# Spreading the experts' factors over the partitions: by a transfer from DRAM instead of by TensorE

## The chip, the cores and the metric

The kernel runs on one core of a Trainium2 chip. The metric is the time of one execution on the device in microseconds; the runs shown are three of the same kernel, and one further execution was profiled. A core has TensorE (PE; its loads of weights are shown apart as PEld), VectorE (DVE), ScalarE (ACT), GpSimd (POOL) and SyncE (SP, which here only issues transfers). SBUF is the memory on the core, PSUM the one that TensorE writes.

## What is computed

Four layers, each of an attention and a mixture or a gated network, each followed by a residual sum and a layer norm, for 1024 tokens of width 256. The change concerns the last mixture and the routing that prepares it:

```python
logits = jnp.dot(h, router_w.T)                      # 1024 x 64 experts
probs = jax.nn.softmax(logits, axis=-1)
top_vals, top_idx = lax.top_k(probs, 8)
top_vals = top_vals / jnp.sum(top_vals, axis=-1, keepdims=True)
comb = jnp.zeros((T, E)).at[jnp.arange(T)[:, None], top_idx].add(top_vals)
def body(acc, xs):                                   # over the 64 experts
    wgu, wd, w_e = xs                                # 64 units each
    g, u = jnp.split(jnp.dot(h, wgu.T), 2, axis=-1)
    eo = jnp.dot(jax.nn.silu(g) * u, wd.T)
    return (acc + eo * w_e[:, None], None)
shared = sigmoid(h @ shared_expert_gate_w.T) * ((silu(h @ sg.T) * (h @ su.T)) @ sd.T)
x = _layernorm(x + expert_out + shared)
```

The kernel computes all experts for all tokens, each hidden unit multiplied by the factor that its expert has for that token (zero where the expert isn't among the 8). The gate of the shared expert is a 65th factor.

## The kernel before

The tokens are eight tiles of 128; two halves of 512 columns serve as the moving operand. The hidden units lie on the partitions: a chunk is a pair of experts (2 x 64 units), the 33rd chunk is the shared expert (64 units). A unit of work, `add_up(i, half)` in `ffn`, makes gate and up of one chunk for one half (line 159, two fp32 matmuls each), calls `hidden`, and adds the product with the down weights to the accumulators (line 307, two fp32 matmuls). The profile shows each fp32 matmul as two records. `ffn` runs the first half of chunk i and then the second half of chunk i - LAG, with LAG = 3.

**Factors.** While the attention ends, `close(t)` finishes two token tiles at a time (t = 0, 2, 4, 6): norm, transposes (line 178), router matmuls (line 166), softmax, top 8, and the factors `comb`. It is a generator of 11 steps. `close_on` runs one step per unit of the attention, one closing after the other; what is left is run by `ffn` through its argument `before`, one step after each gate and each up, and all the rest when i = LAG - 1 is through (the flush). The last steps split the factors into three bfloat16 parts (`split3`, lines 363 to 365, on VectorE; two groups of 33 factors) and transpose them (`transpose_comb`, line 353) into `combT`, two tiles of 99 rows (3 parts x 33) and 1024 columns.

**Spread.** In `hidden`, a unit needs the factor of its expert on each of its 64 partitions. GpSimd copies columns of a selection matrix (line 2249), and one bfloat16 matmul with it as weights (`spread`, line 1100) adds the three parts up and puts each factor on its 64 partitions, in a bank of PSUM. ScalarE computes Silu of the gate (line 2255), VectorE multiplies by up (line 2256) and by the factors (line 2257).

**Buffers and order.** PSUM has four banks for gate, up and spread, and four for the accumulators. The weights come by transfers on SP's queue into a pool `w` of 10 tiles, of which `combT` holds two. The order of the instructions in the attention is the written one on all engines, SP too; in the last mixture a scheduler orders each engine's instructions at compile time by the program's order and by what is ready in its model. So line 307 of a unit stands behind the gate of the next one. Each engine runs its own list in order.

Of the kernel before, what the change touches and what calls it, by code (L numbers as in the profile page):

```python
# [24 lines left out]
BF16 = mybir.dt.bfloat16  # L25
# [3 lines left out]
ALU = mybir.AluOpType  # L29
AX = mybir.AxisListType  # L30

P = 128
T = 1024
# [3 lines left out]
HALF = 512  # L37
# [5 lines left out]
class Kit:  # L43
# [242 lines left out]

    LAG = 3

    def ffn(self, chunks, count, hidden, before=iter(())):

        nc = self.nc
        acc = [self.wide() for _ in range(NC)]
        held = {}

        def add_up(i, half):
            size, gate, up, down, more = held[i] if half == 0 else held.pop(i)
            g, u = self.bank()[:size], self.bank()[:size]  # L300
            self.project(g, gate, half * HALF, HALF)
            next(before, None)
            self.project(u, up, half * HALF, HALF)
            next(before, None)
            h = hidden(g, u, half, more)
            for m in range(NC):
                nc.tensor.matmul(  # L307
                    acc[m][:, half * HALF : (half + 1) * HALF],
                    lhsT=down[:, m * P : (m + 1) * P], rhs=h, start=i == 0, stop=i == count - 1,
                )  # L310

        for i in range(count + self.LAG):
            if i < count:
                held[i] = next(chunks)
                add_up(i, 0)
            if i == self.LAG - 1:
                for _ in before:
                    pass
            if i == count - 1:
                self.add_ffn(acc, 0)  # L320
            if i >= self.LAG:
                add_up(i - self.LAG, 1)
        self.add_ffn(acc, 1)

    def add_ffn(self, acc, half, scale=None):
# [19 lines left out]
                )  # L345
        self.norm_half(half)

    def transpose_comb(self, parts, combT, t):

        n = combT.shape[0]  # L350
        ps = self.bank()[:n, : 2 * P]
        for i in range(2):
            self.nc.tensor.transpose(
                ps[:, i * P : (i + 1) * P], parts[:, i].rearrange("p s e -> p (s e)"), self.ident
            )
        self.nc.vector.tensor_copy(combT[:, t * P : (t + 2) * P], ps)

    def split3(self, parts, x, shape):

        nc = self.nc  # L360
        short = self.tile("st", shape, BF16, tag="short", bufs=2)
        for i in range(2):
            nc.vector.tensor_copy(short, x)
            nc.vector.tensor_copy(parts[i], short)
            nc.vector.tensor_tensor(parts[2], x, short, ALU.subtract)
            x = parts[2]

    def selector(self, n):

        t = self.tile("st", [3 * n, n], BF16, tag=f"select{n}", bufs=1)  # L370
        for i in range(3):

            cols = self.ident[: 3 * n, i * n : (i + 1) * n]
            if i == 0:
                self.nc.gpsimd.tensor_copy(t, cols)
            else:
                self.nc.gpsimd.tensor_tensor(t, t, cols, ALU.add)
        return t

class Pair:  # L380

# [67 lines left out]
class Pipe:  # L449
# [6 lines left out]
    LAG = 5  # L456
# [436 lines left out]
def ffn0(k, a):  # L893
# [198 lines left out]
                if not late and tile_ + 2 < len(ternary_tiles):  # L1092
                    next(ternary_tiles[tile_ + 2])
    k.moe = results, slots, prob


def spread(k, select, combT, half):

    by = k.bank()[: select.shape[1]]
    k.nc.tensor.matmul(  # L1100
        by, lhsT=select, rhs=combT[:, half * HALF : (half + 1) * HALF], start=True, stop=True
    )
    return by


def attn1(k, a):
# [832 lines left out]
def attn3(k, a):  # L1939

    nc = k.nc
# [21 lines left out]
    for _ in load(0):  # L1963
# [4 lines left out]
        out=wr[:, :, :64], in_=a["L3_ffn_router_w"].rearrange("(c p) e -> p c e", p=P)  # L1968
    )
    nc.sync.dma_start(out=wr[:, :, 64], in_=a["L3_ffn_shared_expert_gate_w"])  # L1970
    k.combT = [k.tile("w", [99, T], BF16) for _ in range(2)]
    k.closing, stats = [], {}

    def close(t):
# [26 lines left out]
        for i in range(2):  # L2001
# [6 lines left out]
        nc.vector.tensor_reduce(total, probs, axis=AX.X, op=ALU.add)  # L2008
        nc.vector.reciprocal(inv, total)


        comb = k.tile("t2", [P, 2, 2, 33])
        nc.vector.tensor_tensor(
            comb[:, :, :, :32], probs.rearrange("p t (g e) -> p t g e", g=2),
            inv.unsqueeze(2).unsqueeze(3).to_broadcast([P, 2, 2, 32]), ALU.mult,
        )
        nc.gpsimd.memset(comb[:, :, 0, 32], 0.0)
        nc.vector.tensor_scalar(gate, gate, 1.0, None, ALU.add)
        nc.vector.reciprocal(comb[:, :, 1, 32], gate)
        parts = [k.tile("t2", [P, 2, 3, 33]) for _ in range(2)]  # L2020
        for group in range(2):
            yield
            k.split3(
                [parts[group][:, :, i, :] for i in range(3)], comb[:, :, group, :], [P, 2, 33]
            )
        for group in range(2):
            yield
            k.transpose_comb(parts[group], k.combT[group], t)

    def close_on():  # L2030
        if k.closing and next(k.closing[0], k) is k:
# [182 lines left out]
def ffn3(k, a):  # L2214


    nc = k.nc
    select = k.selector(33)

    def chunks():  # L2220
        gu = wd = None
        for p in range(32):
            if p % 2 == 0:
                gu = k.weights(
                    [P, NC, 512],
                    a["L3_ffn_gate_up"][:, p * 256 : (p + 2) * 256].rearrange(
                        "(c p) f -> p c f", p=P
                    ),
                )
            if p % 4 == 0:  # L2230
                wd = k.weights([P, 4, D], a["L3_ffn_down"][:, p * D : (p + 4) * D])
            at = (p % 2) * 256
            yield (
                P, lambda c, w=gu, s=slice(at, at + P): w[:, c, s],
                lambda c, w=gu, s=slice(at + P, at + 2 * P): w[:, c, s], wd[:, p % 4, :], p,
            )
        gu = k.weights([P, NC, P], a["L3_ffn_shared_gate_up"].rearrange("(c p) f -> p c f", p=P))
        wd = k.weights([64, D], a["L3_ffn_shared_down"])
        yield (64, lambda c: gu[:, c, :64], lambda c: gu[:, c, 64:], wd, 32)

    chosen = {}

    def hidden(g, u, half, p):
        n = g.shape[0]
        group, at = (1, 32) if n == 64 else (p // 16, p % 16 * 2)
        if half == 0:

            chosen[p] = k.tile("t2", [99, n], BF16, tag="t1", bufs=4)
            nc.gpsimd.tensor_copy(  # L2249
                chosen[p].rearrange("r (e u) -> r e u", u=64),  # L2250
                select[:, at : at + n // 64].unsqueeze(2).to_broadcast([99, n // 64, 64]),
            )
        by = spread(k, chosen[p], k.combT[group], half)
        s, h = (k.tile("t2", [P, HALF])[:n] for _ in range(2))
        nc.scalar.activation(s, g, AF.Silu)  # L2255
        nc.vector.tensor_tensor(h, s, u, ALU.mult)  # L2256
        nc.vector.tensor_tensor(h, by, h, ALU.mult)
        return h

    k.ffn(chunks(), 33, hidden, (step for steps in k.closing for step in steps))  # L2260


STAGES = (attn0, ffn0, attn1, ffn1, attn2, ffn2, attn3, ffn3)
# [5 lines left out]
    attn2: dict(wide=3, q=4, k=4, v=2, pt=3, ot=6, tops=2, parts=6),  # L2269
    ffn2: dict(p4=3, t2=8),  # L2270
    attn3: dict(q=12, k=4, v=8, pt=2, p4=2, turned=2, ot=3, t2=4, raw=2),
    ffn3: dict(p4=4, t2=8),
}


# [89 lines left out]
```

## Time and profile before

| | |
|---|---|
| runs shown | 2253.94, 2241.89, 2248.37 us; median 2248.37 |
| profiled execution | 2254.7 us, span of its profile 2253.0 us |
| mean granted clock of TensorE | 0.962 |
| busy over the span | PE 2060.1 us (91%), DVE 1306.5 (58%), ACT 851.0 (38%), POOL 532.1 (24%) |
| transfers | 169.57 MB, mean 75 GB/s; SP's queue 24.9% of 16 engines' span |
| last mixture | from 1868 us to the end |

The page gives the busy time of each engine, the span in 40 slices, the transfers, the chain of work that ended last, and the costliest groups of instructions by line. A row of the timeline is: start, duration, engine, line, operation, output and inputs with their shapes, count, and in brackets the idle time before it with what ended it. Matmuls are pipelined and overlap in it; the distance between starts is the time that one costs. A row of the table of windows is: the window, its length, then busy time and number of instructions of PE, PEld, DVE, ACT and POOL, the granted clock, the mean busy share of the 16 DMA engines, and GB/s. A row of the transfers is: output and input, queue, kind, count, KB of each, and the median time from issue to landing.

### The profile page before, as it was taken

How to read it: one execution, taken by the hardware profiler on the slowest of the kernel's cores; microseconds unless marked ns; L12 is line 12 of the kernel's file. 1: busy time of each engine (PE TensorE's matmuls, PEld its weight loads, DVE VectorE, ACT ScalarE, POOL GpSimd, SP SyncE). 2: the span in 40 equal slices, each digit the busy share in tenths (PEclk: the TensorE clock that was granted, in tenths of full speed). 3: DMA queues.
4: the chain of work that ended last, by engine and by line, in shares of the span. 5: the costliest groups of instructions: out<-in, count | busy, mean ns of one | idle time of the engine just before them, and what ended most of it. 6: DMA issues, size and time to landing. Idle time of an engine off the chain costs nothing.

```text
span 2253.0 us, 24727 instructions
## 1 busy us (share of the span) xinstructions
PE 2060.1 (91%) x7967; PEld 1211.3 (54%) x7967; DVE 1306.5 (58%) x2640; ACT 851.0 (38%) x2232; POOL 532.1 (24%) x811
## 2 busy tenths in 40 slices
PE   7988777899999997988988998899999988999997
PEld 4656544566666665754444443466666664444443
DVE  6898756577777664555664445277777664222223
ACT  3656424443444433444353222654444432111111
POOL 5343132233333323312110000333333320000000
PEclk9999879899999998989999999999999999999998
DMA  6322543154546543015000000044444330111100
GB/s 184 72 71 57 145 125 107 49 144 109 145 100 159 142 104 83 24 43 169 11 2 10 29 28 2 24 94 110 92 106 98 75 106 19 38 37 47 31 1 19
DMA packets 143728, 169.57 MB, mean 75 GB/s; under 512 B 31248, under 2 KB 114768, under 8 KB 143600
## 3 DMA queue, kind: packets, MB, share of 16 engines
q1 hardware_dynamic: 134016, 142.95, 24.9%
q0 software_dynamic: 9584, 25.05, 3.6%
q8 instruction: 64, 1.05, 0.2%
q14 instruction: 64, 0.52, 0.1%
HBM read 68.20 MB, written 17.17 MB: 38 GB/s over the span
## 4 chain that ended last, share of the span: by engine, by line
PE 66%; DVE 9%; ACT 3%; DMA 3%; issue 3%; POOL 2%; SPq 1%; DVEq 0%; ACTq 0%; POOLq 0%
PE bank L159 22%; PE wide L274 9%; PE bank L439 8%; PE wide L307 8%; PE bank L166 4%; DVE turned L402 2%; PE bank L1219 2%; DMA pt<-turned 2%; PE bank L887 2%; PE bank L1656 2%; PE bank L1394 1%; PE bank L1050 1%; ACT pt L1681 1%; PE wide L1669 1%; POOL p L267 1%
## 5 line engine op out<-in xcount | busy, mean ns | idle before, releaser
L159 PE MATMUL bank<-xT,w 128*128 128x512 f32 (+1 forms) x1488 | 644.9, 567 | 6.3 <-DVE xT L185 6.0
L159 PEld LDWEIGHTS bank<-xT,w 128*128 128x128 f32 x1488 | 286.5, 196 | 272.9 <-issue 248.0
L402 DVE STREAM_TRANSPOSE turned<-p 128x128 f32<-128x128 f32 (+7 forms) x232 | 283.6, 1222 | 83.3 <-DMA pt<-turned 47.5
L274 PE MATMUL wide<-k,q 128*128 128x512 f32 (+3 forms) x768 | 295.3, 494 | 18.4 <-ACT p L259 17.5
L267 POOL TENSOR_SCALAR p<-p,st 128x128 f32<-128x128 f32 (+7 forms) x256 | 190.3, 743 | 486.0 <-DVE st L266 485.4
L439 PE MATMUL bank<-pt,v 128*128 128x256 f32 x1216 | 281.5, 373 | 12.1 <-DMA pt<-turned 7.8
L439 PEld LDWEIGHTS bank<-pt,v 128*128 128x128 f32 x1216 | 227.2, 192 | 65.6 <-issue 24.2
L254 DVE TENSOR_REDUCE st<-wide 128x1 f32<-128x128 f32 (+7 forms) x256 | 193.4, 756 | 50.8 <-PE wide L279 43.8
L274 PEld LDWEIGHTS wide<-k,q 128*128 128x128 f32 x768 | 140.1, 192 | 135.8 <-issue 93.2
L307 PE MATMUL wide<-t,w 128*128 128x512 f32 x392 | 189.0, 605 | 8.0 <-DVE t L1933 4.8
L2256 DVE TENSOR_TENSOR t<-t,bank 128x512 f32<-128x512 f32 x66 | 45.3, 687 | 246.6 <-PE bank L159 246.6
L259 ACT ACTIVATE p<-wide,st,factor 128x128 f32<-128x128 f32 (+7 forms) x128 | 106.3, 830 | 214.6 <-POOL st L256 213.0
L259 ACT ACTIVATE p<-wide,st 128x128 f32<-128x128 f32 (+7 forms) x128 | 94.8, 740 | 234.9 <-DVE st L254 213.9
L2255 ACT ACTIVATE t<-bank 128x512 f32<-128x512 f32 x66 | 39.4, 597 | 292.5 <-PE bank L159 287.7
L307 PEld LDWEIGHTS wide<-t,w 128*128 128x128 f32 x392 | 68.3, 189 | 112.7 <-issue 48.3
L166 PE MATMUL bank<-w,xT 128*128 128x512 f32 (+2 forms) x288 | 118.6, 549 | 0.8 <-DVE st L266 0.8
L810 ACT ACTIVATE e<-wide,st 128x128 f32<-128x128 f32 x256 | 89.8, 376 | 75.6 <-DVE st L818 67.1
L249 DVE TENSOR_TENSOR wide<-wide,causal 128x128 f32<-128x128 f32 x192 | 55.8, 291 | 97.1 <-PE wide L274 96.0
L1681 ACT ACTIVATE pt<-wide 128x1024 f32<-128x1024 f32 (+3 forms) x96 | 75.6, 811 | 70.3 <-PE wide L1675 68.5
L2249 POOL COPY t<-select 99x128 bf16<-99x128 bf16 (+1 forms) x33 | 9.4, 291 | 318.2 <-PE bank L1100 318.2
L166 PEld LDWEIGHTS bank<-w,xT 128*128 128x128 f32 x288 | 52.6, 196 | 46.2 <-issue 40.0
L1633 DVE TENSOR_REDUCE st<-wide 128x2 f32<-128x1024 f32 x64 | 64.3, 1020 | 21.2 <-PE wide L1629 10.3
(316 smaller groups left out, 2918.1 us busy)
## 6 DMA issues: line engine op xcount, KB each, us to landing
pt<-turned SPq DMA_DIRECT2D x60, 240.0 KB, 4.8
pt<-turned SPq DMA_DIRECT2D x60, 176.0 KB, 3.5
pt<-turned SPq DMA_DIRECT2D x156, 64.0 KB, 2.1
w<-in_L_ffn_gate_up_dram SPq DMA_DIRECT2D x16, 512.0 KB, 3.7
pt<-turned SPq DMA_DIRECT2D x28, 256.0 KB, 4.8
pt<-turned SPq DMA_DIRECT2D x60, 112.0 KB, 2.9
pt<-turned SPq DMA_DIRECT2D x28, 224.0 KB, 4.2
w<-in_L_attn_Wq_dram SPq DMA_DIRECT2D x12, 512.0 KB, 3.8
```

The source lines that it names most:

```text
L159: self.nc.tensor.matmul(out, lhsT=weight(c), rhs=self.xcols(c, lo, n), start=c == 0, stop=c == NC - 1)
L166: self.nc.tensor.matmul(out, lhsT=self.xcols(c, lo, n), rhs=weight(c), start=c == 0, stop=c == NC - 1)
L254: nc.vector.tensor_reduce(top, scores[:, :n], axis=AX.X, op=ALU.max, negate=True)
L259: nc.scalar.activation(probs[:, :n], scores[:, :n], AF.Exp, bias=top, scale=1.0 if scale is None else scale, accum_out=total,)
L267: self.nc.gpsimd.tensor_scalar(probs[:, :n], probs[:, :n], total, 1.0, ALU.mult, ALU.mult)
L274: self.nc.tensor.matmul(s[:, lo : lo + m], lhsT=query, rhs=key(lo, m), start=True, stop=not masked or lo + m < n, skip_group_check=masked,)
L307: nc.tensor.matmul(acc[m][:, half * HALF : (half + 1) * HALF], lhsT=down[:, m * P : (m + 1) * P], rhs=h, start=i == 0, stop=i == count - 1,)
L402: k.nc.vector.transpose(squares.rearrange("p b (k q) -> p b k q", q=32), probs[:, :n].rearrange("p (k i b) -> p b k i", b=4, i=32),)
L439: self.k.nc.tensor.matmul(out.rearrange("p (a q) -> p a q", q=32) if first else out.rearrange("p (s a q) -> p s a q", s=2, q=32), lhsT=val ...
L810: nc.scalar.activation(e[:, r, f, b, :], sc[:, r, f, b, :], AF.Exp, bias=top[:, at : at + 1], accum_out=total[:, at : at + 1],)
L1633: nc.vector.tensor_reduce(st[:, i, :] if half else to, sc[:, :, :n], axis=AX.X, op=ALU.max, negate=True,)
L1681: nc.scalar.activation(two[:, :, lo:], sc[:, :, lo:], AF.Exp)
```

## The change

The factors stay in float32. `close` transposes them directly (65 rows: 64 experts and the shared gate) and stores them in a tensor `factors` of [65, 1024] in DRAM, by a transfer on SP's queue. The steps of splitting go; a closing has 9 steps, one of them empty. In `hidden`, a transfer on SP's queue reads the rows of the chunk's experts, repeats each over 64 partitions, and lands in a new tile `by` in SBUF, of which there are 8. `split3`, `transpose_comb`, `selector`, `spread` and `combT` go. `ffn` gets its lag as an argument, and the last mixture uses 4.

```diff
-    def ffn(self, chunks, count, hidden, before=iter(())):
+    def ffn(self, chunks, count, hidden, before=iter(()), lag=LAG):
...
-            if i == self.LAG - 1:
+            if i == lag - 1:
                 for _ in before:
                     pass
...
-            if i >= self.LAG:
-                add_up(i - self.LAG, 1)
+            if i >= lag:
+                add_up(i - lag, 1)
...
-    k.combT = [k.tile("w", [99, T], BF16) for _ in range(2)]
+    k.factors = k.tile("dram", [65, T], tag="factors")
...
-        comb = k.tile("t2", [P, 2, 2, 33])
+        comb = k.tile("t2", [P, 2, 65])
         nc.vector.tensor_tensor(
-            comb[:, :, :, :32], probs.rearrange("p t (g e) -> p t g e", g=2),
-            inv.unsqueeze(2).unsqueeze(3).to_broadcast([P, 2, 2, 32]), ALU.mult,
-        )
-        nc.gpsimd.memset(comb[:, :, 0, 32], 0.0)
+            comb[:, :, :64], probs, inv.unsqueeze(2).to_broadcast(shape), ALU.mult
+        )
         nc.vector.tensor_scalar(gate, gate, 1.0, None, ALU.add)
-        nc.vector.reciprocal(comb[:, :, 1, 32], gate)
-        parts = [k.tile("t2", [P, 2, 3, 33]) for _ in range(2)]
-        for group in range(2):
-            yield
-            k.split3(
-                [parts[group][:, :, i, :] for i in range(3)], comb[:, :, group, :], [P, 2, 33]
-            )
-        for group in range(2):
-            yield
-            k.transpose_comb(parts[group], k.combT[group], t)
+        nc.vector.reciprocal(comb[:, :, 64], gate)
+        yield
+        yield
+        ps = k.bank()[:65, : 2 * P]
+        for i in range(2):
+            nc.tensor.transpose(ps[:, i * P : (i + 1) * P], comb[:, i, :], k.ident)
+        combT = k.tile("t2", [65, 2 * P])
+        nc.vector.tensor_copy(combT, ps)
+        nc.sync.dma_start(out=k.factors[:, t * P : (t + 2) * P], in_=combT)
...
     def hidden(g, u, half, p):
         n = g.shape[0]
-        group, at = (1, 32) if n == 64 else (p // 16, p % 16 * 2)
-        if half == 0:
-            chosen[p] = k.tile("t2", [99, n], BF16, tag="t1", bufs=4)
-            nc.gpsimd.tensor_copy(
-                chosen[p].rearrange("r (e u) -> r e u", u=64),
-                select[:, at : at + n // 64].unsqueeze(2).to_broadcast([99, n // 64, 64]),
-            )
-        by = spread(k, chosen[p], k.combT[group], half)
+        by = k.tile("by", [P, HALF])[:n]
+        rows = k.factors[2 * p : 2 * p + n // 64, half * HALF : (half + 1) * HALF]
+        nc.sync.dma_start(out=by, in_=rows.unsqueeze(1).to_broadcast([n // 64, 64, HALF]))
...
-    k.ffn(chunks(), 33, hidden, (step for steps in k.closing for step in steps))
+    k.ffn(chunks(), 33, hidden, (step for steps in k.closing for step in steps), lag=4)
...
-    ffn3: dict(p4=4, t2=8),
+    ffn3: dict(p4=4, t2=8, by=8),
```

## The prediction

> **What bounds the kernel now.** I read the table of windows first, for the stage; then the timeline of one steady unit, for the wait that ends last; then the timeline of the stage's first units; then the transfers.
>
> ```profile
> 1850.00:2253.00 403.00, 382.90 (x987) 172.29 (x985) 123.40 (x275) 56.20 (x91) 11.18 (x35) 0.98 0.09 28
> ```
>
> The last mixture starts at 1868 (its first L159) and is bound by TensorE (382.9 of 403 us busy; VectorE 123, ScalarE 56, GpSimd 11, transfers 9%). So relief for GpSimd or ScalarE is worth nothing here. One unit (a pair of experts, one half of the tokens) in steady state:
>
> ```profile
> 2001.15 1.88 PE L159 MATMUL bank<-xT,w 128*128 128x512 f32 x4
> 2002.87 0.38 PE L1100 MATMUL bank<-w,t 99*128 99x512 bf16 x1
> 2003.09 1.88 PE L159 MATMUL bank<-xT,w 128*128 128x512 f32 x4
> 2003.14 0.69 DVE L2256 TENSOR_TENSOR t<-t,bank 128x512 f32<-128x512 f32 x1 [3.89 <-PE bank L159]
> 2003.93 0.69 DVE L2257 TENSOR_TENSOR t<-bank,t 128x512 f32<-128x512 f32 x1
> 2004.68 0.32 PEld L307 LDWEIGHTS wide<-t,w 128*128 128x128 f32 x2 [0.54 <-DVE t L2257]
> 2004.81 1.88 PE L307 MATMUL wide<-t,w 128*128 128x512 f32 x4
> 2006.52 1.88 PE L159 MATMUL bank<-xT,w 128*128 128x512 f32 x4
> 2008.24 0.38 PE L1100 MATMUL bank<-w,t 99*128 99x512 bf16 x1
> ```
>
> Starts count, not busy times. Four records (two fp32 matmuls) take 1.72 us from start to start; the bf16 spread (L1100) takes 0.22 (2002.87 to 2003.09), though it is shown as 0.38. A unit is 3 x 1.72 + 0.22 = 5.37 us, which is the distance between two spreads. See also how tight L307 sits: up ends at 2002.87, L2256 and L2257 follow, L307 loads its weights at 2004.68 and starts at 2004.81, at once when the next gate (started 2003.09) is through. VectorE is a second chain with almost no slack.
>
> The start of the stage holds the only long idle of TensorE:
>
> ```profile
> 1887.78 1.00 PE L166 MATMUL bank<-w,xT 128*128 128x65 f32 x8
> 1894.01 1.18 PE L353 MATMUL bank<-ident,t 128*99 128x128 f32 x4 [5.23 <-DVE t L365]
> 1894.98 6.02 PE L159 MATMUL bank<-xT,w 128*128 128x512 f32 x8
> ```
>
> The router of the last two token tiles (L166) is followed by 5.23 us in which TensorE waits for softmax, top 8 and split on VectorE, and then eight records take 6.02 us instead of 3.6.
>
> Transfers in three windows (the last two columns are the busy share of 16 DMA engines and GB/s): a plain 256 KB transfer at 448, and at 506 the two loads of scales, whose source is 8 rows, each repeated 16 times, so that its outermost dimension is 8:
>
> ```profile
> 448.00:448.50 0.50, 0.50 (x5) 0.45 (x4) 0.41 (x2) 0.00 (x0) 0.00 (x0) 1.00 0.98 377
> 506.00:506.50 0.50, 0.50 (x4) 0.45 (x3) 0.50 (x1) 0.50 (x1) 0.00 (x0) 1.00 0.50 197
> 506.50:507.00 0.50, 0.50 (x3) 0.26 (x2) 0.50 (x1) 0.50 (x3) 0.00 (x0) 1.00 0.50 132
> ```
>
> The repeated rows kept exactly half of the engines busy. A busy engine moves 377 / (0.98 x 16) = 24.0 GB/s in the plain transfer, 164.5 / 8 = 20.6 in the other.
>
> **The Trainium skill.** (1) "DMA: Bandwidth & Descriptors", section "Why a DMA increments its semaphore by 16 and not by 1": the number of engines of one DMA is the largest one up to 16 that divides the slowest dimension (other than 1) of both access patterns. The windows at 506 agree (8 of 128 partitions: 8 engines), though those were issued by GpSimd; no run yet shows a smaller one from SP. (2) "TensorE: Matmul & The Clock Gate", Part 1: after about 3.4 us idle the clock is halved until TensorE has been busy for about as long; the 6.02 us agree. (3) "VectorE: DVE Perf Modes", "Why tensor_tensor can't do 2×_2P or 4×": two fp32 tensors go at the plain rate from SBUF also. The trace agrees: 0.724 us for 128x512 with both in SBUF (L191), 0.692 for L2257 with one in PSUM.
>
> **The change, part by part.** The sum is made against the profiled execution (2254.7 us, span 2253.0), which lies 0.3% above the median 2248.37; I carry the difference over.
>
> *Spread leaves TensorE.* 66 x 0.22 = 14.2 us of issue. But L307 still waits for L2256 and L2257. From the end of up to L307's earliest start: 0.27 + 0.79 + 0.75 and about 0.12 for the weights = 1.92 us; the next gate now fills 1.72 of it. So 0.20 of the 0.22 turns into a wait for L2257, unless the scheduler puts half of the next up ahead of L307. Value: 0 to -14 us, taken -1.
>
> *GpSimd* loses 33 copies (9.4 us, hidden under 318 us of idle): nothing.
>
> *Split goes.* Per pair of tiles 12 VectorE instructions of about 0.2 us and 2 of 4 transposes go; one copy of 0.42 and one transfer of 65 KB come. Behind L166 that shortens the chain by 1.3 us (1892.7 to 1894.0). More important, a closing falls from 11 steps to 9, and lag=4 lets two more steps run before the flush. Counting steps: before, the pair t=4 enters the stage with 8 steps left and t=6 with all its router work in the flush. After, t=4 enters with 2 left, t=6 gets its router matmuls after the third unit's up, and its softmax runs beside the fourth unit's gate and up (3.4 us). The 5.23 us and the 2.4 us of half clock should mostly go: -8 us (0 to -9, since a new order may leave the wait). In the attention's tail, three split instructions (1.0 us) lie inside one wait of 2.9 us before L421: 0 to -1.
>
> *The store* sits on SP in the fixed order of the attention; it waits for the copy, and the `pt<-turned` transfers behind it wait for later work of VectorE anyway: nothing, at most 0.5 us each.
>
> *The spread by DMA.* 64 transfers of 256 KB (and two of 128 KB). Their source is [2, 64, 512]: outermost dimension 2, so by (1) **two engines of 16**, the same two each time, 128 KB each. At 24.0 GB/s that is 5.46 us, at 20.6 it is 6.36; the second rate contains a transfer's start, so I weigh 2 to 1: 5.73 us. All loads of weights pass these two engines as well:
>
> ```profile
> w<-in_L_ffn_gate_up_dram SPq DMA_DIRECT2D x12, 512.0 KB, 3.7
> w<-in_L_ffn_down_dram SPq DMA_DIRECT2D x6, 512.0 KB, 3.6
> ```
>
> 18 x 32 KB at 24.0 = 25 us. Together 64 x 5.73 + 25 = 392 us on each of the two, against 5.35 x 66 = 353 us of TensorE. Eight buffers give a lead, not a rate. The first transfer can start when the factors of tiles 0 to 3 are stored: the transposes of t=2 now lie about where its step 7 lay (1853), plus copy, store and landing: 1857; if the loads are issued only with the stage, 1868. I take 1862. Then the last pair's factors land at 1862 + 392 = 2254. After that come L2257 (0.75), two L307 (3.4) and what followed L307 before (2241.8 to 2253.0, 11.2): 15.4 us, so 2269: **+16 us**. What TensorE gained (the -1 and -8) is cover that this queue eats; it isn't added. SP issues 66 more transfers of some 0.37 us (as for gate_up), 24 us in 380; each may wait for a buffer, and weights behind it wait too, which costs no more since they share the queue.
>
> **The rivals.**
> *A, the transfer is hidden*: the framework or the queue spreads it over 16 engines (1.4 us per unit). Then TensorE's terms count: -1 - 8 - 1 = -10, to -24 where the order also removes the wait for L2257: 2224 to 2238, about 2235. For it: 9% transfer load today. Against: the half share at 506.
> *B, two engines at the plain rate from 1857*: 1857 + 64 x 5.46 + 25 = 2231, end 2247, -6: **2242, no difference**. For it: 24.0 GB/s was seen in an undisturbed transfer. The point from which the queue costs time is 5.56 us per transfer with this start (5.48 with mine).
> *C, two engines reading the same row 64 times are as slow as the loads of scales*: start 1866, 64 x 6.36 + 25 = 2298, end 2313, +60: 2309.
>
> **Numbers.** About 0.5% (11 us) is what a measurement of this kernel can tell from no change. Forecast, slower, 2264: 0.41; C 0.10; B 0.20; A 0.29. So faster 0.29, same 0.20, slower 0.51. The likeliest case alone reaches from 2255 to 2285. The range goes from 2230 (most of A) to 2300 (short of C).
>
> **What would show it.** Right: the loads of `by` take over 5 us each and keep about 2/16 = 0.13 of the engines busy through the whole stage (weights on top); L307 or L2257 waits for the transfer of `by`; the units lie 5.8 us or more apart; TensorE's idle behind L166 is gone. B: the same shares, with units near 5.5. A: landings of 2 to 4 us, units at 5.35 with L307 waiting for L2257, or at 5.15 with no wait. Wrong altogether: a tail of the attention that moved by more than 3 us, or factors that arrive late only in the first units.

## The result, and the profile after

The kernel after takes 2237.87 us (median of 20 runs) against 2248.13 us of the kernel before (20 runs): ratio 0.9952, 95% interval 0.9944 to 0.9961, so 0.5% **faster** (10.3 us by the medians, 10.8 by the ratio). The forecast was 16 us slower. The profiled execution of after took 2230.2 us (span 2228.5).

Single executions differ by more than this change: up to the last attention, TensorE's instructions are the same in both kernels, and yet the profile of after is 16.8 us ahead there (1384.4 against 1401.2). So I compare stages. From its first L159 to the end of the span, the last mixture took 384.9 us before (from 1868.13) and takes 379.8 us after (from 1848.71). The last attention takes 464.3 us against 466.9.

In the kernel after, line 2201 loads `by`, 2203 is Silu, 2204 and 2205 are the products with up and with the factors, 1981 transposes the factors; 159, 166, 178 and 307 are as before. First the window of the last mixture (columns as before: window, length, busy time of PE, PEld, DVE, ACT and POOL, clock, share of DMA engines, GB/s):

```profile
1830.00:2228.00 398.00, 375.74 (x916) 163.82 (x916) 114.82 (x223) 54.06 (x89) 2.56 (x4) 0.98 0.21 70
```

TensorE is still nearly full, and the transfers rose from 9% to 21%. The next two windows hold nothing but loads of `by`; the table of transfers counts them:

```profile
1900.00:1910.00 10.00, 10.00 (x24) 4.12 (x23) 2.76 (x4) 1.19 (x2) 0.00 (x0) 1.00 0.13 51
1950.00:1960.00 10.00, 10.00 (x24) 4.21 (x23) 2.24 (x4) 1.19 (x2) 0.00 (x0) 1.00 0.13 51
```

```profile
by<-factors SPq DMA_DIRECT2D x64, 256.0 KB
```

A share of 0.13 is 2 of 16 engines, as forecast. But these two move 51 GB/s, 25.5 each, so a transfer takes 262144 B / 51 GB/s = 5.14 us; the packet records of the trace have 5.13 us between the ends of two. I had taken 5.73.

A steady unit early in the stage (timeline, DVE, ACT and PE):

```profile
1910.04 3.60 PE L159 MATMUL bank<-xT,w 128*128 128x512 f32 x8
...
1912.02 0.69 DVE L2204 TENSOR_TENSOR t<-t,bank 128x512 f32<-128x512 f32 x1 [3.86 <-PE bank L159]
1912.74 0.69 DVE L2205 TENSOR_TENSOR t<-by,t 128x512 f32<-128x512 f32 x1
1913.49 1.98 PE L307 MATMUL wide<-t,w 128*128 128x512 f32 x4
...
1915.31 1.88 PE L159 MATMUL bank<-xT,w 128*128 128x512 f32 x4
```

Eight records are up of this unit and gate of the next. Units lie 5.27 us apart (1910.04 to 1915.31), not 5.37 and not the 5.15 of three times 1.72: L307 takes 1.82 us from start to the next start instead of 1.72, since its first load of weights stands behind the wait for L2205, which ends at 1913.43 just as the gate is through. From 1961 to 2140, while weights are loaded too, 12 of some 33 units look like this:

```profile
2006.20 0.69 DVE L2205 TENSOR_TENSOR t<-by,t 128x512 f32<-128x512 f32 x1 [1.11 <-DMA by<-factors]
2006.95 1.98 PE L307 MATMUL wide<-t,w 128*128 128x512 f32 x4 [0.94 <-DVE t L2205]
```

And the waits of the whole kernel (engine, tile, line, releaser: us in total, times, longest):

```profile
DVE t L2205 <- DMA by<-factors: 12.6, 20, 1.8
PE wide L307 <- DVE t L2205: 11.8, 14, 1.6
```

Two of the 14 waits for L2205 are no work of the queue: they are 1.56 us each, at 2184 and 2215, behind the shared expert at the end of each half, and e1 below has them too. So the queue costs TensorE 8.7 us of waits here. After 2140 there are no weights left to load, and no more of these. At the start of the stage the idle stretch is gone: the timeline has the last pair's router at 1863.42 and its transposes six microseconds later with no idle before them, at full clock:

```profile
1863.42 1.00 PE L166 MATMUL bank<-w,xT 128*128 128x65 f32 x8
1864.26 2.79 PE L159 MATMUL bank<-xT,w 128*128 128x512 f32 x6
...
1869.46 0.38 PE L1981 MATMUL bank<-ident,t 128*65 128x128 f32 x2
```

### The profile page after: what moved, and what is told of

It is laid out like the page before. It is cut to its first block, busy times and chain, and to the rows that moved or that the text cites. A ratio compares the mean times of both kernels' runs of the same rounds, so it can differ in the third digit from the quotient of the medians.

```text
span 2228.5 us, 24592 instructions
## 1 busy us (share of the span) xinstructions
PE 2037.2 (91%) x7893; PEld 1191.4 (53%) x7893; DVE 1299.4 (58%) x2588; ACT 849.6 (38%) x2230; POOL 522.3 (23%) x771
## 4 chain that ended last, share of the span: by engine, by line
PE 62%; DVE 9%; DMA 7%; ACT 3%; issue 3%; POOL 2%; SPq 1%; DVEq 0%; POOLq 0%; ACTq 0%
PE bank L159 19%; PE wide L274 9%; PE bank L408 8%; PE wide L307 6%; DMA by<-factors 5%; PE bank L166 4%; PE bank L1179 2%; DVE turned L371 2%; PE bank L1616 2%; PE bank L856 2%; PE bank L1019 1%; DMA pt<-turned 1%; PE bank L1354 1%; POOL p L267 1%; PE wide L1629 1%
## 5 line engine op out<-in xcount | busy, mean ns | idle before, releaser
L159 PE MATMUL bank<-xT,w 128*128 128x512 f32 (+2 forms) x1488 | 629.2, 563 | 4.1 <-DVE xT L185 3.0
L159 PEld LDWEIGHTS bank<-xT,w 128*128 128x128 f32 (+1 forms) x1488 | 283.1, 194 | 275.1 <-issue 254.3
L307 PE MATMUL wide<-t,w 128*128 128x512 f32 (+1 forms) x392 | 196.7, 626 | 17.0 <-DVE t L2205 11.8
L2204 DVE TENSOR_TENSOR t<-t,bank 128x512 f32<-128x512 f32 (+1 forms) x66 | 45.3, 686 | 238.8 <-PE bank L159 238.8
L2203 ACT ACTIVATE t<-bank 128x512 f32<-128x512 f32 (+1 forms) x66 | 39.4, 597 | 305.5 <-PE bank L159 279.5
L307 PEld LDWEIGHTS wide<-t,w 128*128 128x128 f32 (+1 forms) x392 | 67.8, 191 | 134.3 <-DVE t L2205 58.4
L845 PE MATMUL bank<-w,ot 128*128 128x256 f32 x256 | 67.4, 411 | 6.8 <-ACT ot L839 5.5
```

The lines of the kernel that those rows point to most:

```text
L159: self.nc.tensor.matmul(out, lhsT=weight(c), rhs=self.xcols(c, lo, n), start=c == 0, stop=c == NC - 1)
L307: nc.tensor.matmul(acc[m][:, half * HALF : (half + 1) * HALF], lhsT=down[:, m * P : (m + 1) * P], rhs=h, start=i == 0, stop=i == count - 1,)
L845: nc.tensor.matmul(y, lhsT=oT[:, i % 2 * 2 + i // 2].rearrange("p b n -> p (b n)"), rhs=wo[:, i, :], start=i == 0, stop=i == 3,)
```

## The experiments

Two figures for each kernel: the ratio to the kernel before on the same chip, and the length of the last mixture in its profile (first L159, or what stands for it, to the end of the span). "Rest" is what the time changed by outside that stage: (ratio - 1) x 2248, less the change of the stage from 384.9. Each length is that of one profiled execution; kernels that do the same in this stage agree within 1.2 us (before and e18; after and e14). The last column is where the tiles allocated in the last stages begin, in bytes past a multiple of 256 (factors / tiles of earlier stages).

| kernel | ratio, 95% | last mixture, us | rest, us | place |
|---|---|---|---|---|
| before | 1 | 384.9 | 0 | - / 160 |
| after | 0.9952 (0.9944 to 0.9961) | 379.8 | -5.7 | 0 / 0 |
| e1_sixteen | 0.9886 (0.9867 to 0.9905) | 366.1 | -6.8 | 0 / 0 |
| e2_factor_first | 0.9954 (0.9939 to 0.9970) | 378.8 | -4.2 | 0 / 0 |
| e3_both | 0.9909 (0.9890 to 0.9928) | 367.9 | -3.5 | 0 / 0 |
| e4_before_nine | 0.9984 (0.9970 to 0.9998) | 376.9 | +4.4 | - / 160 |
| e5_eleven_lag3 | 0.9977 (0.9967 to 0.9986) | 386.2 | -6.5 | 0 / 0 |
| e6_extra | 1.0122 (1.0103 to 1.0141) | 421.2 | -8.9 | 0 / 0 |
| e7_by16 | 1.0027 (1.0015 to 1.0039) | 395.5 | -4.5 | 0 / 0 |
| e8_turned | **0.9852** (0.9832 to 0.9872) | 357.6 | -6.0 | 0 / 0 |
| e9_turned_product | 0.9877 (0.9859 to 0.9896) | 366.0 | -8.8 | 0 / 0 |
| e10_turned_two | 0.9932 (0.9918 to 0.9945) | 376.4 | -6.8 | 0 / 0 |
| e12_before_lag4 | 1.0005 (0.9994 to 1.0016) | 385.7 | +0.3 | - / 160 |
| e13_two_queues | 1.0041 (1.0029 to 1.0054) | 400.8 | -6.7 | 0 / 0 |
| e14_held | 0.9956 (0.9940 to 0.9972) | 380.9 | -5.9 | 0 / 0 |
| e16_selector | 1.0016 (1.0007 to 1.0025) | 388.6 | -0.1 | 96 / 96 |
| e17_after_pad32 | 1.0041 (1.0026 to 1.0057) | 396.5 | -2.4 | 32 / 32 |
| e18_before_pad32 | 0.9996 (0.9985 to 1.0007) | 385.5 | -1.5 | - / 192 |
| e19_after_pad64 | 1.0017 (1.0008 to 1.0025) | 389.4 | -0.7 | 64 / 64 |
| e20_pad_last | 1.0023 (1.0013 to 1.0032) | 395.5 | -5.4 | 32 / 0 |

### Does the queue on two engines cost time?

**e1_sixteen**: one transfer per expert.

```diff
-        rows = k.factors[2 * p : 2 * p + n // 64, half * HALF : (half + 1) * HALF]
-        nc.sync.dma_start(out=by, in_=rows.unsqueeze(1).to_broadcast([n // 64, 64, HALF]))
+        for e in range(n // 64):
+            row = k.factors[2 * p + e : 2 * p + e + 1, half * HALF : (half + 1) * HALF]
+            nc.sync.dma_start(out=by[64 * e : 64 * e + 64], in_=row.to_broadcast([64, HALF]))
```

> The kernel after, but each expert's 64 partitions are loaded by a transfer of their own (outermost dimension 64), so that all 16 DMA engines should share it. Theory (the queue on two engines still costs time after the change): the 12.6 us in which VectorE waits for the factors vanish, units lie 5.27 us apart to the end of the stage, and the time is 9 to 12 us below the kernel after, near 2227; the share of busy engines outside the weight loads is no longer 0.13. Rival (the two-engine transfer is hidden, and its waits only stand in the place of others): within 3 us of the kernel after, near 2237.

Measured: 13.7 us less in the stage than after, and 0.9886 against 0.9952. Units lie 5.27 to 5.28 us apart to the end of the stage, VectorE never waits for `by`, and a transfer lands 2.9 us after its issue (median). The theory holds, and the effect is somewhat above the 9 to 12 us that it named. Two down matmuls one unit apart:

```profile
2001.19 1.98 PE L307 MATMUL wide<-t,w 128*128 128x512 f32 x4
2006.46 1.98 PE L307 MATMUL wide<-t,w 128*128 128x512 f32 x4
```

The view of the tile `by` has no entry under "sat idle before it":

```profile
L2202 SPq DMA_DIRECT2D by<-factors x130: 444/588/597, 1851.9 to 2170.0; - x130
L2206 DVE TENSOR_TENSOR t<-by,t x66: 678/691/693, 1867.8 to 2215.7; 128x512 f32<-128x512 f32 x64, 64x512 f32<-64x512 f32 x2
its engine sat idle before it (us, times) until:
```

**e6_extra**: the kernel after with 12% more on the same two engines.

```diff
+        more = k.tile("more", [16, HALF])[: 8 * (n // 64)]
+        nc.sync.dma_start(out=more, in_=rows.unsqueeze(1).to_broadcast([n // 64, 8, HALF]))
```

> The kernel after, with a second small transfer behind each load of the factors: the same rows onto 16 partitions of a tile that nobody reads (outermost dimension 2, 8 rows of 2 KB more on each of the same two engines), which raises the load per unit from 5.13 us to 72/64 x 5.13 = 5.77 us, about what the prediction took for it. Theory (the two engines end the stage, and the prediction failed by the size of the transfer): about 58 x 0.64 = 37 us above the kernel after less what TensorE hides, near 2268; units at 5.8 us and more. Rival (the waits for the factors have another cause, such as SP's order): less than 10 us above the kernel after.

Measured: the stage 41.4 us longer than after; the waits of VectorE for `by` go from 12.6 to 41.7 us. That is 65 us per us of transfer, about one for each of the 66 units: the queue is what ends there. With a load of 5.77 us per unit, about what I forecast for a transfer, the kernel is 27 us slower than before, more than the 16 that were forecast.

**e13_two_queues**: half of the transfers on ScalarE's queue (`(nc.sync, nc.scalar)[half].dma_start`).

> The kernel after, with the factors of the second half of the tokens loaded through ScalarE's queue and those of the first half through SP's. Open is whether a second queue's transfers of outermost dimension 2 use the same two engines. Theory 1 (the same two engines): VectorE's waits for the factors stay near 12 us or grow, since ScalarE now also waits for free buffers ahead of Silu: 0 to +8 us against the kernel after. Theory 2 (other engines, or the rate is that of the queue and not of the engines): the waits fall under 3 us, and the time is 8 to 12 us below the kernel after, near 2228.

Measured: 21 us longer than after in the stage. While transfers of both queues are under way a window still shows

```profile
1950.00:1960.00 10.00, 10.00 (x24) 4.12 (x23) 2.76 (x4) 0.60 (x1) 0.00 (x0) 1.00 0.13 51
```

that is, the same two engines. The Trainium skill, "DMA: Bandwidth & Descriptors", section "Issuing engines are not separate DMA queues", says that transfers of any issuing engine run on the same 16; this run agrees, and for a transfer of two rows it is the same 2 of the 16. The loss was larger than theory 1 allowed, since ScalarE now stands in front of Silu with a transfer that waits for a buffer (three waits of L2203 with 32.5 us in all).

**e7_by16**: `by=16` instead of `by=8`.

> The kernel after with 16 buffers for the spread factors instead of 8. Theory (rate: with the weight loads the two engines need 5.13 + 23/64 = 5.49 us a unit, against 5.27 of TensorE, and the lead is set by when the last tokens' factors are stored): no change, 0 to -3 us, waits for the factors still over 9 us. Rival (lead: the queue stood still for lack of free buffers early in the stage): the waits fall to 5 us or less, -7 us and more.

Measured: neither. The waits for `by` are gone altogether, so there was lead to be had, and the stage is 15.7 us longer. The waits list shows what came late instead:

```profile
PE bank L159 <- DMA w<-in_L_ffn_gate_up_dram: 14.0, 4, 6.2
PE wide L307 <- DMA w<-in_L_ffn_down_dram: 7.3, 1, 7.3
```

The queue gave its lead to `by`, and the weights, which stand behind in the same list, arrive late: TensorE waits 21.3 us for weights, where in after it waited 8.7 us for the factors. The rest of the 15.7 us goes with the half clock behind the longest of these waits (granted clock of the stage 0.962, against 0.980 in after). More buffers for the one load are a delay for the other where both share a bound queue.

### What did TensorE gain?

**e4_before_nine**: the kernel before, with split and spread kept, closings of 9 steps and lag=4.

```diff
+        yield
         for group in range(2):
-            yield
             k.split3(...)
+        yield
         for group in range(2):
-            yield
             k.transpose_comb(parts[group], k.combT[group], t)
...
-tag="t1", bufs=4)
+tag="t1", bufs=5)
```

> The kernel before with split and spread on TensorE, but the closings cut from 11 steps to 9 (both splits in one step, both transposes in another) and lag=4 (with five buffers for the spread 0/1 rows instead of four). Theory (the shorter closings and the later flush removed the idle stretch of TensorE at the start of the stage): the wait of 5.23 us behind the router and the half clock after it go, -8 us against the kernel before, near 2240. Rival (the idle went because the split went from VectorE): the wait stays at 3 us or more, and the time is within 3 us of the kernel before.

Measured: the stage is 8.0 us shorter, as worked out, and the wait of 5.23 us behind the router and the half clock are gone (the longest wait left at the start is 1.47 us). The whole kernel gains 3.6 us only. In its profile the attention is 7.9 us longer than before; TensorE waits there for both splits that now come in one piece, and longer for the attention's own probabilities (`p`):

```profile
1810.04 0.46 PE L353 MATMUL bank<-ident,t 128*99 128x128 f32 x2 [1.29 <-DVE t L365]
...
1854.96 1.97 PE L421 MATMUL bank<-ident,p 128*128 128x128 f32 x8 [3.42 <-POOL p L267]
```

**e12_before_lag4**: lag=4 alone.

> The kernel before with lag=4 alone (and five buffers for the spread 0/1 rows), closings of 11 steps as they were. Theory (the gain at the start of the stage needs the shorter closings, since with 11 steps the last pair's router still falls into the flush behind the fourth unit): the wait of about 5 us behind the router stays, 0 to -2 us against the kernel before. Rival (the later flush is what removes it): the wait falls below 2 us, and -6 us or more.

Measured: no gain (385.7), and the long wait is there, 6.66 us. The lag alone doesn't do it; the shorter closings are needed. Whether they would do it with lag=3 was not tried.

```profile
1892.23 1.15 PE L353 MATMUL bank<-ident,t 128*99 128x128 f32 x4 [6.66 <-DVE t L365]
```

**e5_eleven_lag3**: the kernel after with two more empty `yield` in `close` and lag=3.

> The kernel after, with two more empty steps in each closing (11 again) and lag=3 (the factors still spread by DMA). Theory (the shorter closings and the later flush are worth about 7 us at the start of the stage, whatever spreads the factors): TensorE's wait in front of the transposes of the last factors is back at 3 us or more and half clock follows; Silu of the first unit to Silu of the last takes 5 to 8 us longer than in the kernel after, or less by what the transfers then gain in lead (the waits for the factors, 12.6 us, may shrink); time 2238 to 2245. Rival (steps are worth nothing here since the queue of transfers ends the stage): within 2 us of the kernel after.

Measured: 6.4 us more in the stage, and the wait is back, though shorter than before, since no split stands in it:

```profile
1882.37 0.69 PE L1983 MATMUL bank<-ident,t 128*65 128x128 f32 x2 [3.85 <-DVE t L1972]
```

So the steps are worth 6.4 to 8.0 us on either side of the change. What else the change does to TensorE is the distance from e4 to e1: 376.9 - 366.1 = 10.8 us. Of it 66 x (5.37 - 5.275) = 6.3 us is the steady unit; the rest, 4.5 us, lies at the start of the stage, where e4 still waits for splits (1.1 us) and makes twice the transposes; how the 4.5 us divide was not measured.

### What is left in the unit: the products behind up

**e2_factor_first** multiplies Silu by the factors first and by up last (`h = by * s`, then `h * u`); **e3_both** does it on top of e1.

> The kernel after, but VectorE multiplies Silu(gate) with the factors first and with up last, so that only one VectorE instruction (0.69 us) lies between the end of up and the down matmuls. The scheduler then puts the down matmuls half a gate (0.86 us) after up, not a whole one (1.72 us). Theory (the queue on two engines binds in the later part of the stage): little, 0 to -4 us against the kernel after, with VectorE still waiting for the factors, now in the first of the two products. Rival 1 (the wait of the down matmuls for the second product is what the change is short of): units at 5.15 us and -8 us. Rival 2 (the earlier place of the down matmuls brings a new wait of about 0.2 us per unit): 0 to +6 us.

> The kernel after with both edits: one transfer per expert over 16 engines, and the factors multiplied first. Theory (queue first, the chain on VectorE second): 8 us below the variant with 16 engines alone, units at 5.15 us, near 2219. Rival (down matmuls only half a gate after up: 0.20 for up's landing + 0.69 + 0.12 for the weights against 0.86): units at 5.25 to 5.35, within 4 us of the variant with 16 engines alone, near 2227.

Measured: e2 within 0.5 us of after (0.9954 against 0.9952), e3 1.9 us longer than e1 in the stage. In both the units lie 5.34 us apart, as in e3:

```profile
2004.99 1.98 PE L307 MATMUL wide<-t,w 128*128 128x512 f32 x4
2010.33 1.98 PE L307 MATMUL wide<-t,w 128*128 128x512 f32 x4
```

The scheduler, expecting the product earlier, put L307 behind half a gate, and the new wait (5.34 - 5.15 = 0.19 us) is longer than the old one (0.13). The rival of e3 and the second of e2 were right about the units. So the order has to be held as well.

**e8_turned**: e3 with the order of the steady units written out, the down matmuls of a unit behind the whole gate of the next.

```diff
             self.project(g, gate, half * HALF, HALF)
+            while late:
+                late.pop()()          # the down matmuls of the unit before
...
+            late.append(down_matmuls)
+            if not turned[0]:
+                late.pop()()
...
+            with self.in_order():
+                turned[0] = True
+                for i in range(lag, count - 1):
+                    step(i)
```

> The variant with 16 engines, the factors multiplied before up, and the order of the steady units written out: the down matmuls of a unit stand behind the whole next gate (1.72 us after up's end). Theory (the remaining wait per unit is the chain of two VectorE products: 0.20 for up's landing + 2 x 0.75 + weights against 1.72): with one product, no wait, units at 3 x 1.715 = 5.15 us instead of 5.27, 62 x 0.13 = 8 us below the variant with 16 engines alone, near 2220. Rival (the 0.13 us is a cost of changing between matrices on TensorE that no order removes): units stay at 5.27 and the time near 2228.

Measured: units at 5.15 us, the stage 8.5 us below e1, ratio 0.9852: 33 us faster than before and 22 us faster than after, the fastest kernel of this study. The down matmuls (line 311 here) now take their 1.72 us:

```profile
2001.87 1.88 PE L311 MATMUL wide<-t,w 128*128 128x512 f32 x4
2003.58 3.60 PE L159 MATMUL bank<-xT,w 128*128 128x512 f32 x8
2007.02 1.88 PE L311 MATMUL wide<-t,w 128*128 128x512 f32 x4
```

**e9_turned_product**: the same order with up first and the factors last.

> The variant with 16 engines and the steady units' order written out as in the fastest variant so far (2215), but with VectorE's products as in the kernel after (up first, factors last, both behind up). A control for where that variant's 0.13 us a unit came from. Theory (the chain of two VectorE products behind up): units at 5.27 us as with 16 engines alone, and the time near 2228, 12 us above the fastest variant. Rival (the written order itself): units at 5.15 us, near 2216.

Measured: units at 5.27 us and a stage of 366.0 us, that of e1. So the 0.13 us is the second product behind up, and the written order by itself gives nothing.

**e10_turned_two**: e8 with the two-engine transfer of the kernel after.

> The fastest variant so far (written order, factors multiplied before up, units at 5.15 us), but with the factors loaded as in the kernel after, by one transfer on two engines. Theory (the queue of the two engines ends the stage as soon as it runs out of lead, so TensorE's gain is cover that it eats): units at 5.15 us for the first ones, then VectorE waits for the factors for 18 to 22 us in all instead of 12; the time within 4 us of the kernel after, near 2237, and 20 us above the same kernel with 16 engines. Rival (the waits depend on how units fall, not on the rate): the gain of 0.13 us a unit comes through, near 2228.

Measured: units at 5.15 us until about 1950, then about half of them come late by up to 2 us, with VectorE waiting for `by`; the stage is 376.4 us, 18.8 us above e8 and only 3.4 below after. Of the 8.5 us that the same two edits gain with 16 engines (e8 against e1), the queue eats 5.1.

### Where are the other five microseconds?

The last mixture explains -5.1 of the -10.8 us. Two things outside the last mixture differ: `combT` held two of the weight pool's ten buffers, and GpSimd built a 0/1 matrix at the start.

**e14_held**: after, with two tiles of the weight pool held to the end.

> The kernel after, with two of the weight pool's ten buffers held from the start of the last attention to the end, as the two tiles of split factors held them in the kernel before. The last mixture and the last attention account for about 7 us of the 10.7 us gained; some 4 us lie ahead of them or are spread. Theory 1 (the two freed buffers bring them): near 2242, 4 us above the kernel after. Theory 2 (they come from elsewhere): within 2 us of the kernel after, ratio to before 0.994 to 0.996.

**e16_selector**: after, with `select = k.selector(33)` kept, unread.

> The kernel after, with the 0/1 matrix of the spread still built by GpSimd (three small instructions that the scheduler puts at the start of the kernel, ahead of the masks) and read by nobody. Theory 1 (GpSimd's instructions at the start of the kernel delay the first stages): near 2242, 4 us above the kernel after. Theory 2 (they cost nothing): within 2 us of the kernel after.

Measured: the buffers are nothing (0.9956). The matrix takes all the gain away (1.0016), and not where theory 1 saw it: the last mixture is 8.8 us longer, with 19.7 us of waits for `by`, though only GpSimd's list of instructions has changed: those of TensorE, VectorE and ScalarE are the same, in the same order. What moved are the tiles. The matrix takes 96 bytes of each partition, and everything allocated later lies 96 bytes further: in the built program `by` is at 105568 instead of 105472, which is a multiple of 256 (and of 512). In the kernel before, the matrix and the small tiles of the split push the later tiles by 416 bytes, to 160 past a multiple of 256. The weights' tiles lie ahead of all these and keep their place. So the last four runs moved tiles only; the one small `memset` that comes with each costs nothing by e14, which has four of them.

```diff
+    pad = k.tile("st", [P, 8], tag="pad", bufs=1)       # e17: 32 bytes; e19: [P, 16]; e18: in the kernel before
+    nc.gpsimd.memset(pad[:, :1], 0.0)
...
-    ffn3: dict(p4=4, t2=8, by=8),
+    ffn3: dict(pad=1, p4=4, t2=8, by=8),                # e20: a pool of its own, in the last stage
```

> The kernel after, with a tile of 32 bytes per partition that nobody reads, where the 0/1 matrix of the spread lay. The instructions of every engine stay in their order (one small GpSimd memset at the start); all later tiles move by 32 bytes in SBUF, the spread factors from 105472 (a multiple of 512) to 105504 (32 over a multiple of 64), the place that they had with the 0/1 matrix kept and that the kernel before gives its tiles. Theory (placement): near 2252, as with the 0/1 matrix, ratio to before 1.000 to 1.003, with transfers of factors at 5.2 instead of 5.1 us. Rival (GpSimd's instructions, or chance): within 3 us of the kernel after, ratio 0.994 to 0.997.

> The kernel before, with an unread tile of 32 bytes per partition behind the 0/1 matrix, which moves the later tiles from 32 over a multiple of 64 to a multiple of 64 (105888 to 105920). Theory (placement costs the kernel before in its stages with many transfers into SBUF): -3 to -7 us, ratio 0.997 to 0.9985. Rival: no change, 0.999 to 1.001.

> As the kernel after with 32 bytes of padding, but 64 bytes: the later tiles stay on multiples of 64 (not of 512), and the GpSimd memset is there too. Theory (what counts is a multiple of 64): within 2 us of the kernel after, ratio 0.994 to 0.997. Rival 1 (a larger multiple counts): as with 32 bytes, 1.000 to 1.003. Rival 2 (the memset or any shift costs): likewise 1.000 and more.

> The kernel after, with the unread 32 bytes put into the pools of the last mixture only, so that the factors lie 32 bytes over a multiple of 64 and the tiles of all earlier stages lie as in the kernel after. Theory (placement acts on the queue of the factors as well as on the earlier stages): the last mixture takes 385 to 389 us as with the 0/1 matrix kept, instead of 380; 5 to 8 us above the kernel after, ratio 0.9975 to 0.999. Rival (the placement of the factors does not matter, that of earlier tiles does): within 2 us of the kernel after.

Measured: 32 bytes cost 20 us (1.0041), 64 bytes 14.6 us (1.0017). So a multiple of 64 is not enough, and e18, which went from 160 to 192 bytes past a multiple of 256, shows nothing. e20 moves only the last mixture's own tiles, the factors among them, and its stage is as long as that of e17 within 1.0 us. Its waits and a window with loads of `by` alone:

```profile
DVE t L2207 <- DMA by<-factors: 26.1, 28, 2.1
```

```profile
2180.00:2190.00 10.00, 10.00 (x24) 4.01 (x22) 2.76 (x4) 0.60 (x1) 0.00 (x0) 1.00 0.13 49
```

49 GB/s instead of 51: the packet records have 5.13 us between transfers at a multiple of 256, 5.21 with 96 bytes past it, 5.27 with 64, 5.35 with 32. The stage follows with 379.8, 388.6, 389.4 and 395.5 to 396.5 us. From after to e20 that is 15.7 us for 0.22 us of transfer, 71 per us, near the 65 of e6; from after to e16 it is more, 8.8 us for 0.08.

The Trainium skill, "DMA: Bandwidth & Descriptors", section "How a descriptor splits into AXI transactions", says that a descriptor which does not start at a multiple of 256 bytes is split into one more transaction and fetches bytes that it does not use. The runs agree that it is dearer; that 32 bytes cost more than 96 is not what a count of its unused bytes would give.

The column "rest" falls into two groups: with the earlier stages' tiles at a multiple of 256 it is -3.5 to -8.9 us (13 kernels, mean -6.1), otherwise -2.4 to +4.4 (six kernels beside the kernel before, mean 0.0; the +4.4 is e4 with its longer attention). So the other five or six microseconds come with the place of the earlier tiles too.

The traces of all twenty kernels say where. TensorE's matmul records are the same, in the same order, up to the end of the last attention, so the time between two of them can be compared. From the record at 688.9 us of the kernel after to the one at 952.6 us (most of the second attention and the start of what follows it) the first group takes 263.7 to 269.2 us, mean 266.6, and the second, with the kernel before, 270.5 to 274.2, mean 271.7. Ahead of that stretch the means are 686.0 and 686.9, behind it, up to the end of the last attention, 840.6 and 840.8. In the stretch the packets of `pt<-turned`, whose targets have moved too, are slower in every kernel of the second group: those of 896 bytes take 59.6 to 61.0 ns, against 57.1 to 57.9. That these slower packets are the cause is likely but not shown, since no run moved their tiles alone. Nor was the kernel before run with its tiles at a multiple of 256 bytes: if it gained as much there, only the 5.1 us of the last mixture would be left of the change's gain.

## Why the prediction was wrong

The time went the other way because the queue of two engines, which I had found, is faster than I took it for, and because the place of a tile set its speed. By the steps:

- **Two engines for a transfer of two rows**: right (0.13, in the kernel after and its variants, and from two queues).
- **64 x 5.73 us**: this is the term that failed. It measured 5.13, so it was 38 us too large. I had mixed the plain rate (5.46) with that of the scales' loads (6.36). (Weighted 2 to 1 these give 5.76, not 5.73; the slip is 2 us of the sum.) The 6.36 came from averaging two windows, of which the second holds the start of the next load. The first alone, with 197 GB/s on 8 engines, has 24.6 GB/s per engine, which is 5.32 us, and so showed repeated rows at no lower a rate than plain ones. In the full queue the two engines did a little better still, 25.5 GB/s against 24.0 in the plain transfer; why was not tried. The better price would have been a run of several transfers.
- **The rest of that sum** was 17 us too small, which hid behind the first error. For after it gives, with 5.13, a start 6 us before the stage (1842.6), 64 x 5.13 + 25 and 15.4 behind them: 2211, where the profile ends at 2228.5. The first five transfers did run early (from 1838.09), but no further one ran until 1874, since the next needs the last pair's factors (stored at 1870.78); less five transfers that is a start at 1848.4, 5.8 us later. The weights took 22 us, not 25. And the last factors land near 2198.5, 30 us before the end and not 15.4, because after 2140 the queue is faster than TensorE and runs ahead: 14.6 us. So the break-even was not 5.48 to 5.56 us per transfer either. In e16, with 5.21 us, the stage is already 3.7 us longer than before; a straight line between it and after puts the break-even of the stage near 5.18 us (an estimate).
- **"What TensorE gained is cover that this queue eats; it isn't added"**: wrong as an either-or. Queue and TensorE are so close (5.13 us and the weights against 5.27) that both count: the change gains 8.0 us by the steps and 10.8 by what left TensorE, and the queue takes 13.7 back: -5.1.
- **Spread leaves TensorE**, taken as -1: the mechanism was right (L307 then waits for L2205, as e9 and e8 show), the size was not. 0.13 of the 0.22 us turn into a wait, not 0.20, because the two products start 0.72 us apart and not 0.79; 6.3 us. (The 0.724 us for L191 was a mean of 16 with two long ones, 0.908 and 0.989; its median is 0.693, that of L2205 0.692.)
- **Split goes, steps**, -8: right (e4 -8.0, e5 +6.4), and for the reason given: the softmax of t = 6 runs beside gate and up. The half clock that went was longer than the 3.4 us that I had read: from 1893 to 1900 us of the kernel before the granted clock is 0.51, with TensorE busy for 6.0 of the 7.
- **Attention tail**, 0 to -1: within what the profiles can tell. The attention takes 464.3 us after, 466.9 before, and 465.1 in e12, which has the old code in it.
- **GpSimd: nothing**: its copies, yes. But the small tiles that went with split and spread had pushed every later tile off a multiple of 256 bytes. A step "what moves in SBUF" was missing altogether. It decides the sign: with the last mixture's tiles 32 bytes further the same change is 0.23% slower (e20), with all tiles moved 0.41% (e17).
- **The rivals**: A named TensorE's gains, and the measured 2238 lies in its range, but by luck: the transfer was not hidden, and half of the gain came with the place of the tiles. B was nearest in the rate (5.46 against 5.13), but its break-even rested on the same sum.

## What to carry to other kernels

In these runs a broadcast whose outermost dimension was 2 kept two engines busy, from SP's queue and from ScalarE's; split into transfers with an outermost dimension of 64 (e1), it no longer held anything up. So look at the outermost dimension of a broadcast first. Price a queue that never empties by its rate in a busy stretch, against the engine it feeds, and treat two that are within a few per cent as both counting. When a small tile is dropped or added, look where the others land: keep the targets of a bound transfer at a multiple of 256 bytes, and test a small gain against a kernel that differs only in the place.

## What the runs showed of the hardware that I had not expected

- The place of a target in SBUF changes the time of a transfer of 2 KB rows by up to 4% (5.13 us at a multiple of 256 bytes, 5.35 at 32 bytes past one); a multiple of 64 is not enough (5.27). Multiples of 128 alone were not tried.
- Two engines in a full queue move 51 GB/s, 25.5 each, reading the same 2 KB row 64 times.
- The order of TensorE's instructions that a scheduler writes can turn a shorter chain into no gain at all: one product less behind up, and the matmuls moved up by half a gate to wait again (5.34 us a unit in e2 and e3 against 5.15 in e8).
